# Vision transformer tower: the stacked keys in two tiles of four key chunks each

## The chip, the cores and the metric

The kernel runs on one core of a Trainium2 chip, as a single program. The metric is the device time of one execution in microseconds (us), lower is better. The core has five engines that run side by side, each with its own queue of instructions in a fixed order: TensorE (PE in the profile; its weight loads are PEld), VectorE (DVE), ScalarE (ACT), GpSimd (POOL) and SyncE (SP). SP only issues DMA transfers here, and an instruction that waits on SP holds back all transfers behind it. Instructions wait for each other through semaphores.

## The reference, cut to what matters

Sixteen images of 3 x 512 x 512 are cut into 1024 patches each, and every patch is projected to 256 channels. Then comes one transformer layer with a norm ahead of each part: attention with 8 heads of 32 channels, and a feed-forward part (a shared network, and the two best of four experts). In the attention the keys pass elementwise through a Fourier series of 256 frequencies before they meet the queries:

```python
def _L0_attn_ref(x, w_qkv, w_out, b_out, kan_a, kan_b):
    ...
    q, k, v = (to_heads(q), to_heads(k), to_heads(v))
    k = kan_transform(k, kan_a, kan_b)      # sum_f a_f*sin(f*x) + b_f*cos(f*x), f = 1..256
    scale = HEAD_DIM ** (-0.5)
    dots = jnp.einsum('bhqd,bhkd->bhqk', q, k) * scale
    attn = jax.nn.softmax(dots, axis=-1)
    out = jnp.einsum('bhqk,bhkd->bhqd', attn, v)
    out = out.transpose(0, 2, 1, 3).reshape(b, n, d)
    return out @ w_out + b_out
...
h = _L0_tok_ref(x, L0_tok_W, L0_tok_b)
h = h + _L0_attn_ref(_layernorm(h, axis=-1), ...)
h = h + _L0_ffn_ref(_layernorm(h, axis=-1), ...)
```

All is float32.

## The kernel before, in words

The heads are worked on in pairs: 4 pairs an image, 64 pairs in all, numbered `p` from 0 to 63. The kernel is one long stream without loops on the chip, in which three kinds of work overlap: the Fourier series of the keys of later pairs, the attention of the present pair, and the projections, norms and networks of the images around it.

**The keys.** The angles of an image's keys are written to DRAM (`keys`, tile `ud`) and read back, repeated over partitions, as wave tiles `w` (`load_waves`, two tiles for each of the 32 groups of an image, two transfers of 256 KB for each tile). GpSimd multiplies them by their frequency (`turn_waves`, L1006), ScalarE takes the sine (`sine`, L1016), TensorE mixes them with the coefficients (`mix`, tile `kan`, L1036), VectorE multiplies by the fast waves (`times_fast`, L1050), and TensorE adds up (`add_up`, tile `red`, L1069). After the last sum of a pair, `finish_keys` splits the keys on VectorE into a high and a low part (L615, L616) and stores both to a DRAM tile `kd` with two transfers (L1088).

**The stacked keys.** `stack_keys` (L1098) reads `kd` back into the SBUF tile `k4` of 128 partitions: partitions 0 to 63 hold the high and the low parts of the 32 channels, partitions 64 to 127 the same again, so that one matmul against the stacked queries `q4` (L1115, `stack_queries`, four transfers) forms all products of the parts. In the free dimension `k4` has four rows of 512 columns: two for each head, and of these one for the key chunks 0 to 3 and one for 4 to 7, a chunk being 128 keys. Two transfers of 512 KB fill it, one for each copy. There is one `k4`; it is written again for the next pair once the last score of the present pair has read it.

**The attention.** A pair has two rounds, one for each half of its 1024 queries (`att`, 128 rounds). In a round, for each of eight key chunks `kc`: `score` (L1134) makes two matmuls of 128 keys by 512 queries into a PSUM tile of two banks (`sT`, from the pool `big`, of which there are two, shared with `kan`); `exponential` (L1149) takes the exponential on ScalarE (`es`, five of them); `weigh` (L1167) multiplies with the values and with ones (`av`). After the last chunk VectorE takes the reciprocal and divides (`normalize`, L1191 and L1196). ScalarE changes its table between sine and exponential in each round (L1284 loads the one for the exponential).

**What sets the order.** The order on TensorE is written out in a string, `ORDER`: M is `mix`, R `add_up`, S `score`, W `weigh`, and digits take the next step of one of four chains of the remaining work. The order on the other engines comes from a planner that runs at build time: each step is put in a queue with a cost in us and the steps that it depends on (`put`), and at each point the step that could begin first, by those costs, is laid next (`others`, `heads`). The costs and the `done` times only decide the order of instructions; the waits on the chip come from the tiles that an instruction reads and writes. For `stack_keys` the planner's dependencies are the keys in `kd` and the last score of the pair before; `score` depends on the stacked keys and the queries of its round; `finish_keys` of pair `p` on the stacking of pair `p - 2`, which has read the same one of the two `kd` tiles. Further, a transfer issued on SP waits until the one eight issues before it has landed, because its semaphore is used again.

Of the kernel before, what the change touches and what calls it, by code (L numbers as in the profile page):

```python
# [11 lines left out]
FP = mybir.dt.float32  # L12
# [6 lines left out]
P = 128  # L19
# [4 lines left out]
NT = N // P  # L24
# [17 lines left out]
FPR = mybir.dt.float32r  # L42
# [9 lines left out]
PE, ACT, DVE, POOL, SP = "pe", "act", "dve", "pool", "sp"  # L52
# [38 lines left out]
def plain_path(ctx: ExitStack, tc: tile.TileContext, a: dict, out: bass.AP, verdict: bass.AP):  # L91
# [9 lines left out]
    nc = tc.nc  # L101
# [4 lines left out]
    def pool(name, bufs, space=None):  # L106
        kw = {} if space is None else {"space": space}
        return ctx.enter_context(tc.tile_pool(name=name, bufs=bufs, **kw))

    const = pool("const", 1)  # L110
# [21 lines left out]
    def load(shape, src, name):  # L132
        t = const.tile(shape, FP, tag=name, name=name)
        nc.scalar.dma_start(out=t, in_=src)
        return t
# [33 lines left out]
    half = load([NW5, 2], a["half"], "half")  # L169
    for i in range(4):  # L170
        nc.scalar.dma_start(out=biases[ds((NE + 1) * i, NE), 0, :], in_=a["eb3"])
        nc.scalar.dma_start(
            out=biases[ds((NE + 1) * i + NE, 1), 0, :], in_=a["sb3"].unsqueeze(0)
# [58 lines left out]
    nc.gpsimd.memset(ones32, 1.0)  # L232


    k4 = const.tile([P, 4, 520], FPR, tag="k4", name="k4")
    aT = const.tile([P, 2, N], FP, tag="aT", name="aT")
    hnT = const.tile([P, 2, N], FP, tag="hnT", name="hnT")
    hT_ = const.tile([P, 2, 512], FP, tag="hT", name="hT")
# [13 lines left out]
    done = {}  # L252
# [8 lines left out]
    def put(engine, queue, cost, deps, key, action):  # L261

        queues[engine].setdefault(queue, []).append((cost, deps, key, action))
# [48 lines left out]
    def transfer(took, issue=0.0, ready=0.0):  # L312

        clock[SP] = max(clock[SP], ready) + issue
        now["dma"] = max(now["dma"], clock[SP]) + took
        return now["dma"] + LANDS
# [292 lines left out]
    def split(src, name):  # L609

        hi, lo = (
            rup.tile([P, 512], FPR, tag=tag, name=name + half)
            for tag, half in (("r", "hi"), ("u", "lo"))
        )
        nc.vector.tensor_copy(hi, src)  # L615
        nc.vector.tensor_sub(lo, src, hi.bitcast(FP))  # L616
        return hi.bitcast(FP), lo.bitcast(FP)
# [340 lines left out]
    def load_source(p):  # L958


        def part(j, blk):
            def action():
                if j == blk == 0:
                    sources[p] = srcp.tile([P, 2, 512], INT, tag="src", name="src")
                ud = images[p // NPAIR]["ud"]
                rows = ud[ts(p % NPAIR, 64), :, 0, :].rearrange(
                    "(g j r e) f n -> j r g e f n", j=2, r=2, e=2
                )
                for r in range(2):
                    nc.sync.dma_start(  # L970
                        out=sources[p][ds(64 * j + 32 * blk, 32), r, :],
                        in_=rows[j, r, :, :, :, ts(blk, 512)],
                    )
                landed = transfer(0.4)
                if j == blk == 1:
                    done["source", p] = clock[SP]
                    done["angles", p] = landed

            return action

        deps = rows_of(8 * p) + [("spread", 8 * p - 1) if p > 0 else ("load", 0, 1)]
        for j in range(2):
            for blk in range(2):
                put(SP, "source", 1.4, deps, ("part", p, j, blk), part(j, blk))
# [39 lines left out]
    red = {}  # L1024
# [29 lines left out]
    rows_of_pair = {}  # L1054
# [27 lines left out]
    def finish_keys(p):  # L1082


        def action():
            kd = rows_of_pair["k", p] = kdp.tile([2, P, 512], FP, tag="kd", name="kd")
            for i, x in enumerate(split(rows_of_pair.pop(p), "k")):
                nc.sync.dma_start(out=kd[i], in_=x)  # L1088
            done["kd", p] = transfer(1.4, 1.1, done["keys", p])

        deps = [("red", 4 * p + 3)] + ([("k4", p - 2)] if p > 1 else [])
        put(DVE, "keys", 1.41, deps, ("keys", p), action)

    def stack_keys(p):
        def action():
            src = rows_of_pair.pop(("k", p)).rearrange("i (d q) n -> (i d) q n", q=4)
            for j in range(2):
                nc.sync.dma_start(out=k4.bitcast(FP)[ts(j, 64), :, 0:512], in_=src)  # L1098
            done["stacked", p] = transfer(3.8)

        deps = [("kd", p)] + ([("score", 2 * p - 1, NT - 1)] if p > 0 else [])
        put(SP, "keys", 1.1, deps, ("k4", p), action)

    bands_of_queries = {}

# [23 lines left out]
    def score(att, kc):  # L1129
        def action():  # L1130
            q4 = bands_of_queries[att]
            ps = scores[kc] = big.tile([P, 1024], FP, tag="big", name="sT")
            for s in range(2):
                nc.tensor.matmul(  # L1134
                    out=ps[:, ts(s, 512)],
                    lhsT=k4[:, 2 * s + kc // 4, ts(kc % 4, P)],
                    rhs=q4[:, s, :],
                    start=True,
                    stop=True,
                )  # L1140

        deps = [("stacked", att // 2), ("q4", att)]
        put(PE, "S", 0.47, deps, ("score", att, kc), action)

    def exponential(att, kc):
# [117 lines left out]
    for p in range(total // 8):  # L1263
        load_source(p)
        finish_keys(p)
        stack_keys(p)
    for att in range(ATT):
        stack_queries(att)
        normalize(att)
    for rd in range(B * RI + 2):  # L1270
        groups = range(GS * rd, min(GS * rd + GS, total))
        att = rd - 2
        attends = 0 <= att < ATT
        for g in groups[::2]:
            first = g == groups[0]
            for i, j in ((0, 0), (0, 1), (1, 0), (1, 1), (0, 2), (1, 2)):
                sine(g + i, j, TABLE if first and i == j == 0 else 0.0)
            mix(g)
            mix(g + 1)
            add_up(g // 2)  # L1280

        def table():
            now["table"] = AF.Exp
            nc.scalar.activation(spare[:, 1:2], spare[:, 0:1], AF.Exp)  # L1284

        put(ACT, "fixed", TABLE + 0.2, [], ("table", rd), table)
        for kc in range(NT) if attends else ():
            score(att, kc)
            exponential(att, kc)
            weigh(att, kc)  # L1290
# [590 lines left out]
def vit_layer(tc: tile.TileContext, a: dict, out: bass.AP):  # L1881
    with tc.tile_pool(name="verdict", bufs=1) as vp:
        verdict = vp.tile([1, 1], mybir.dt.int32, tag="verdict", name="verdict")
        plain_path(tc, a, out, verdict)
        bad = tc.nc.values_load(verdict[0:1, 0:1], min_val=0, max_val=1)
        with tc.If(bad > 0):
            general_path(
                tc, *(ap for name, ap in a.items() if name not in PLAIN_ONLY), out
            )
# [149 lines left out]
```

## Time and profile before

| | |
|---|---|
| Time, median of 3 runs | 3939.81 us (3923.31, 3939.81, 3940.42) |
| The profiled execution's own time | 3924.07 us |
| Its span | 3922.5 us, 102737 instructions |
| Granted TensorE clock | 0.994 |
| ScalarE, exponentials L1149 | 1024 of 1022 ns, 1014.3 us |
| TensorE, scores L1134 | 2048 matmuls, 707.6 us |
| GpSimd, waves L1006 (w) | 1024 of 1895 ns, 1923.6 us |
| SP, stacking L1098 | 128 issues of 512 KB, median 592 ns |
| SP, waves L951 | 2048 issues of 256 KB, median 544 ns |
| DMA, mean over the span | 234 GB/s, 80.6% of the engines on SP's queue |

The span is what the profile covers; the time of that execution is 1.6 us more. In a line of the waits, the engine, its line and the tile that it writes come first, then what it waited for, then the total in us, how many times, and the longest. An engine name with a q (SPq) is its sequencer. In the timeline a line has its start, its length, the engine, the line, the operation with its tiles, and in square brackets the idle time of that engine before it and what ended it. The chain that ended last is followed back from the end of the program through whatever released each step.

### The profile page before, as it was taken

How to read it: one execution, taken by the hardware profiler on the slowest of the kernel's cores; microseconds unless marked ns; L12 is line 12 of the kernel's file. 1: busy time of each engine (PE TensorE's matmuls, PEld its weight loads, DVE VectorE, ACT ScalarE, POOL GpSimd, SP SyncE). 2: the span in 40 equal slices, each digit the busy share in tenths (PEclk: the TensorE clock that was granted, in tenths of full speed). 3: DMA queues.
4: the chain of work that ended last, by engine and by line, in shares of the span. 5: the costliest groups of instructions: out<-in, count | busy, mean ns of one | idle time of the engine just before them, and what ended most of it. 6: DMA issues, size and time to landing. Idle time of an engine off the chain costs nothing.

```text
span 3922.5 us, 102737 instructions
## 1 busy us (share of the span) xinstructions
PE 3810.0 (97%) x40337; PEld 1948.9 (50%) x40337; DVE 2531.7 (65%) x4075; ACT 3263.0 (83%) x3939; POOL 3193.6 (81%) x2328
## 2 busy tenths in 40 slices
PE   7899999999999999999999999999999999999998
PEld 4334454554545555455454545545455454544444
DVE  4656757667675766757667675776767767576652
ACT  2788888888888888888888888888888888888983
POOL 3998878788788878879788788878879888888860
PEclk9999999999999999999999999999999999999999
DMA  7987968888787888979889788798878889788860
GB/s 228 281 261 217 278 192 245 259 226 258 220 257 225 237 264 224 259 216 256 235 233 265 212 257 247 224 265 224 262 218 255 247 229 265 216 245 235 221 170 18
DMA packets 587615, 916.51 MB, mean 234 GB/s; under 512 B 58828, under 2 KB 177524, under 8 KB 587124
## 3 DMA queue, kind: packets, MB, share of 16 engines
q1 hardware_dynamic: 580880, 906.98, 80.6%
q8 instruction: 321, 5.26, 0.6%
q10 hardware_dynamic: 6244, 2.88, 0.3%
q14 instruction: 170, 1.39, 0.1%
HBM read 758.64 MB, written 150.99 MB: 232 GB/s over the span
## 4 chain that ended last, share of the span: by engine, by line
PE 66%; DMA 13%; ACT 8%; POOL 5%; DVE 4%; issue 3%; SPq 2%; ACTq 0%; POOLq 0%; DVEq 0%
PE av L1167 17%; PE sT L1134 10%; PE kan L1036 8%; DMA w<-ud 7%; PE red L1069 4%; PE e1p L301 3%; PE tok L301 3%; ACT w L1016 3%; POOL w L1006 3%; PE e3p L301 2%; PE tok L304 2%; DMA k<-kd 2%; PE s1p L301 2%; PE e1p L304 2%; ACT f L1016 2%
## 5 line engine op out<-in xcount | busy, mean ns | idle before, releaser
L1006 POOL TENSOR_TENSOR w<-w,lane 128x1024 int32<-128x1024 int32 x1024 | 1923.6, 1895 | 406.9 <-DMA w<-ud 275.7
L1149 ACT ACTIVATE es<-sT 128x1024 f32<-128x1024 f32 x1024 | 1014.3, 1022 | 357.3 <-PE sT L1134 312.2
L1016 ACT ACTIVATE w<-w 128x1024 f32<-128x1024 int32 x1024 | 1013.4, 1046 | 67.5 <-POOL w L1006 64.3
L1006 POOL TENSOR_TENSOR f<-f,lane 128x1024 int32<-128x1024 int32 x512 | 970.2, 1895 | 102.0 <-DVE f L991 84.8
L1134 PE MATMUL sT<-q,k 128*128 128x512 f32 x2048 | 707.6, 454 | 42.9 <-DMA k<-kd 13.4
L1050 DVE TENSOR_TENSOR f<-kan,f 128x1024 f32<-128x1024 f32 x512 | 605.2, 1214 | 203.1 <-ACT f L1016 116.3
L991 DVE STREAM_SHUFFLE f<-src 128x1024 int32<-128x1024 int32 x512 | 681.3, 1370 | 0.4
L1167 PE MATMUL av<-es,v 128*32 128x256 f32 x8192 | 638.8, 383 | 3.5 <-DVE rc L1208 2.6
L1167 PE MATMUL av<-es,ones 128*32 128x256 f32 x8192 | 630.9, 379 | 0.0
L1036 PE MATMUL kan<-w,coef 64*32 64x512 f32 x8192 | 540.1, 598 | 18.8 <-ACT w L1016 12.6
L1016 ACT ACTIVATE f<-f 128x1024 f32<-128x1024 int32 x512 | 519.0, 1046 | 4.1 <-POOL f L1006 4.1
L1134 PEld LDWEIGHTS sT<-q,k 128*128 128x128 f32 x2048 | 351.2, 190 | 340.0 <-issue 146.0
L1167 PEld LDWEIGHTS av<-es,v 128*32 128x32 f32 x8192 | 235.5, 109 | 343.2 <-issue 236.9
L1167 PEld LDWEIGHTS av<-es,ones 128*32 128x32 f32 x8192 | 267.2, 110 | 176.4 <-issue 1.4
L1191 DVE RECIPROCAL rc<-av 128x256 f32<-128x256 f32 x128 | 224.8, 1756 | 169.5 <-PE av L1167 169.5
L1036 PEld LDWEIGHTS kan<-w,coef 64*32 64x32 f32 x8192 | 129.1, 105 | 313.9 <-issue 133.4
L1069 PE MATMUL red<-f,pack 128*32 128x512 f32 x2048 | 271.0, 602 | 0.0
L301 PE MATMUL tok<-wt,x 128*128 128x256 f32 x768 | 182.1, 389 | 22.1 <-DMA w1s<-in_sW 12.5
L1016 ACT ACT_TABLE_LOAD x128 | 164.2, 1283 | 17.7 <-DMA w<-ud 15.5
L304 PE MATMUL tok<-wt,x 128*32 128x256 f32 x3072 | 178.0, 380 | 0.6 <-DVE h L548 0.6
L301 PEld LDWEIGHTS tok<-wt,x 128*128 128x128 f32 x768 | 147.4, 194 | 57.9 <-DMA w1s<-in_sW 12.4
L513 ACT ACTIVATE hn<-h,less,rstd 128x256 f32<-128x256 f32 x256 | 140.7, 591 | 39.8 <-POOL less L505 39.0
(148 smaller groups left out, 4269.5 us busy)
## 6 DMA issues: line engine op xcount, KB each, us to landing
w<-ud SPq DMA_DIRECT2D x2048, 256.0 KB
q<-qd SPq DMA_DIRECT2D x512, 128.0 KB
k<-kd SPq DMA_DIRECT2D x128, 512.0 KB
x<-in_xT SPq DMA_DIRECT2D x128, 384.0 KB
ud<-u SPq DMA_DIRECT2D x64, 512.0 KB
ud<-ui SPq DMA_DIRECT2D x64, 512.0 KB
src<-ud SPq DMA_DIRECT2D x512, 64.0 KB
qd<-qhi SPq DMA_DIRECT2D x64, 256.0 KB
```

Source lines behind the costliest of these rows:

```text
L301: nc.tensor.matmul(out=out, lhsT=lhsT, rhs=rhs, start=start, stop=stop)
L304: nc.tensor.matmul(out=out[ts(i, 32)], lhsT=lhsT[:, ts(i, 32)], rhs=rhs, start=start, stop=stop)
L991: nc.vector.stream_shuffle(w, sources[g // 8].rearrange("p r n -> p (r n)"), [4 * (g % 8) + i // 8 for i in range(32)],)
L1006: nc.gpsimd.tensor_tensor(w, w, f.to_broadcast([P, N]), ALU.mult)
L1016: nc.scalar.activation(x, w, AF.Sin, scale=TURN * 2.0**-32)
L1036: nc.tensor.matmul(out=ps[ds(64 * j + 32 * blk, 32), ts(r, 512)], lhsT=coef[ts(r, 64)].rearrange("p e f j -> p (e f j)"), rhs=w[ts(r, 64), ...
L1050: nc.vector.tensor_mul(w, kan.pop(g), w)
L1069: nc.tensor.matmul(out=rows_of_pair[p][ts(2 * i + r, 32), :], lhsT=pack[:, ds(PACK0 - 16 * (k % 2) - 2 * (k // 2), 32)], rhs=prod[:, ts(r, ...
L1134: nc.tensor.matmul(out=ps[:, ts(s, 512)], lhsT=k4[:, 2 * s + kc // 4, ts(kc % 4, P)], rhs=q4[:, s, :], start=True, stop=True,)
L1149: nc.scalar.activation(es, scores.pop(kc), AF.Exp, scale=SCALE)
L1167: nc.tensor.matmul(out=acc[0][ts(i, HD), ts(half, 256)], lhsT=ones32 if half else v[:, kc, p % NPAIR, ts(i % 2, HD)], rhs=es[:, ds(512 * ( ...
L1191: nc.vector.reciprocal(rc[0], acc[0][:, 256:512])
```

## The change

`k4` becomes two tiles, one for key chunks 0 to 3 and one for 4 to 7, each with two rows of 512 columns (one for each head). `stack_keys` is called twice for a pair, once for each tile; each call has its own pair of transfers, of 256 KB each, that read every second row of `kd`, its own entry for the planner, and its own condition: the tile may be written again once the last score of the pair before that reads *this tile* is done (chunk 3 or chunk 7 of the pair's second round). A score waits for the tile of its chunk alone. The planner's figures for one call are 0.8 us of SP and 1.9 us of transfer instead of 1.1 and 3.8.

```diff
-    k4 = const.tile([P, 4, 520], FPR, tag="k4", name="k4")
+    k4 = [const.tile([P, 2, 520], FPR, tag=f"k4{i}", name=f"k4{i}") for i in range(2)]
...
-        deps = [("red", 4 * p + 3)] + ([("k4", p - 2)] if p > 1 else [])
+        deps = [("red", 4 * p + 3)] + ([("k4", p - 2, 1)] if p > 1 else [])
         put(DVE, "keys", 1.41, deps, ("keys", p), action)
 
-    def stack_keys(p):
+    def stack_keys(p, half):
+
         def action():
-            src = rows_of_pair.pop(("k", p)).rearrange("i (d q) n -> (i d) q n", q=4)
+            src = rows_of_pair["k", p].rearrange("i (d s h) n -> h (i d) s n", s=2, h=2)[half]
             for j in range(2):
-                nc.sync.dma_start(out=k4.bitcast(FP)[ts(j, 64), :, 0:512], in_=src)
-            done["stacked", p] = transfer(3.8)
-
-        deps = [("kd", p)] + ([("score", 2 * p - 1, NT - 1)] if p > 0 else [])
-        put(SP, "keys", 1.1, deps, ("k4", p), action)
+                nc.sync.dma_start(out=k4[half].bitcast(FP)[ts(j, 64), :, 0:512], in_=src)
+            done["stacked", p, half] = transfer(1.9)
+
+        deps = [("kd", p)] + ([("score", 2 * p - 1, 4 * half + 3)] if p > 0 else [])
+        put(SP, "keys", 0.8, deps, ("k4", p, half), action)
...
-                    lhsT=k4[:, 2 * s + kc // 4, ts(kc % 4, P)],
+                    lhsT=k4[kc // 4][:, s, ts(kc % 4, P)],
...
-        deps = [("stacked", att // 2), ("q4", att)]
+        deps = [("stacked", att // 2, kc // 4), ("q4", att)]
         put(PE, "S", 0.47, deps, ("score", att, kc), action)
...
     for p in range(total // 8):
         load_source(p)
         finish_keys(p)
-        stack_keys(p)
+        for half in range(2):
+            stack_keys(p, half)
```

In the built program the order on TensorE is the same. On SP the two pairs of transfers of a key pair mostly stand next to each other where the one pair stood; in pairs 2 and 3 four wave loads stand between them, in pair 56 an output store, and in pair 58 two stores of queries.

## The prediction

> **What bounds the kernel now.** I read the page first (busy shares, chain that ended last), then the waits of the engines and of SP's queue, then everything that touches the stacked keys, and last the timeline around single key pairs.
>
> From the page of the kernel before:
>
> ```profile
> PE 3810.0 (97%) x40337; PEld 1948.9 (50%) x40337; DVE 2531.7 (65%) x4075; ACT 3263.0 (83%) x3939; POOL 3193.6 (81%) x2328
> ...
> PE 66%; DMA 13%; ACT 8%; POOL 5%; DVE 4%; issue 3%; SPq 2%; ACTq 0%; POOLq 0%; DVEq 0%
> ```
>
> TensorE is idle for only 3922.5 - 3810.0 = 112.5 us of the span (and its busy ends are modelled), so no change to a wait of TensorE can take more than that; a third of the chain runs through other engines and transfers. The loads of the keys (k<-kd) are 2.1% of the chain, ten visits of 6 to 9 us, each a whole time from issue to landing, and not the idle time that they cause.
>
> From the answers on waits, the engines' and then the queue of SP's (us in total, times, longest):
>
> ```profile
> POOL w L1006 <- DMA w<-ud: 275.7, 98, 9.8
> ...
> PE sT L1134 <- DMA k<-kd: 13.4, 10, 2.4
> ```
> ```profile
> SPq L951 <- PE kan L1036: 228.3, 114, 8.9
> ...
> SPq L1098 <- DMA kd<-klo: 121.1, 60, 4.7
> ...
> SPq L951 <- DMA k<-kd: 30.5, 32, 2.8
> ...
> SPq L1098 <- PE sT L1134: 6.5, 2, 4.6
> ```
>
> The last view decides most. The stacking loads (L1098) wait 60 times for their own source, the keys just written to kd, and 2 times for the scores that still read the old keys. So releasing half of k4 earlier starts almost nothing earlier: the loads stand behind kd. What the change can shorten is the landing, since the first scores now need half the bytes.
>
> Where that matters is in the timeline. Pair 22, SP's queue, TensorE and ScalarE:
>
> ```profile
> 1412.39 0.33 SPq L1088 DMA_DIRECT2D kd<-klo  x1
> ...
> 1418.56 1.42 SPq L1098 DMA_DIRECT2D k<-kd  x2
> 1423.22 5.78 SPq L951 DMA_DIRECT2D w<-ud  x8
> ```
> ```profile
> 1428.60 0.70 PE L1134 MATMUL sT<-q,k 128*128 128x512 f32 x2 [1.57 <-DMA k<-kd]
> ...
> 1432.30 0.61 PE L1167 MATMUL av<-es,v 128*32 128x256 f32 x8
> ```
> ```profile
> 1429.23 1.28 ACT L1284 ACT_TABLE_LOAD   x1
> 1430.52 0.20 ACT L1284 ACTIVATE few<-few 128x1 f32<-128x1 f32 x1
> 1430.63 1.98 ACT L1149 ACTIVATE es<-sT 128x1024 f32<-128x1024 f32 x2
> ```
>
> The two loads are issued at 1418.56, land 7.0 and 9.9 us later by the trace's semaphore records, and the first score starts 0.14 us after the second. I set this beside each other of the 64 pairs. In 17 the first score starts within 0.14 us of the landing; the idle time of TensorE before these sums to 21.0 us (the ten that the waits view names, 13.4 us, and seven put down to a VectorE event that fell in the same moment). Eleven of the 17 are every fourth pair, 14 to 54: there four query loads and two query stores stand between the keys' store and the stacking. In the other 47 the keys land 0.5 to 9.6 us before they are needed. The fifth key chunk, first to read the second half, comes 4.2 to 11.4 us after the first.
>
> **What the Trainium skill says.** Its page Perfetto Trace Analysis, section DMA Instruction — HWDGE, says that the profiled window of a DMA instruction leaves the data movement out. The trace agrees: 0.59 us per L1098 row, landings from 4.8 us. DMA: Bandwidth & Descriptors, section Rules for kernel authors, says that two transfers to disjoint halves serialize on the same engines. It agrees too: the second load lands 2.4 to 3.0 us after the first, with 512 KB each, so splitting saves no bandwidth but orders the bytes. Perfetto Trace Analysis, Identifying Dependency Chains, says that an instruction waiting on several engines can have event-semaphore instructions put ahead of it; the trace has 1104 on TensorE at 51 ns each.
>
> **The change part by part.** All sums are against the profiled execution, 3924.07 us (span 3922.5); the median shown is 15.7 us above it, and I carry the difference over.
>
> *First half sooner.* Four loads of 256 KB replace two of 512 KB; each still has rows of 2 KB. At the spacing of 2.4 to 3.0 us per 512 KB, the first pair of halves lands where one old load did, 2.4 to 3.0 us sooner, and that covers every one of the 17 idles (longest 2.35). But what follows has another condition. The first weighting (av) needs the first exponential, which in pair 22 starts 0.11 us after ScalarE has reloaded its table and ends 1431.64; av starts at 1432.30. ScalarE was busy with sines until 1429.2, so a score 1.57 us earlier moves av by at most 0.6. I credit each pair with the smaller of its idle and this slack: pairs 14, 34, 42, 54 nothing, 38 0.15, 50 0.25, 18 0.55, 22 and 46 0.6, 26 1.0, 30 2.35: 5.5 us. Of the six others, pair 0 has 1.3, 1 0.1, 4 none, 8 0.3, 59 1.4, and 63, the last, 1.8: 4.9. Sum 10.4 us; bounds 0 (ScalarE or a later wait takes it all) and 21.0 (all of it arrives).
>
> *Second half.* Lands at most about 1 us after the old second load (two more issues ahead of it), needed 4 us or more later: nothing. In pairs 2 and 3 the planner now lays four wave loads between the halves; at the 8.8 us of pair 2 plus 4 x 1.1 us for their 256 KB each it lands at 13.2 us against a need at 13.7: nothing, at worst 1 us each. In pair 56 an output store and in 58 two query stores come between; those pairs had 6.1 and 1.7 us of slack.
>
> *Two more waits on TensorE per pair.* Chunk 4 now waits for two transfers besides ScalarE: 64 x 2 x 51 ns = 6.5 us at most, none if TensorE was to wait for ScalarE there anyway. I take 3.
>
> *SP's queue.* Two more issues per pair. The nearest row of this size is w<-ud (256 KB, 544 ns median) and the present L1098 row has 592 ns; four at 0.54 with gaps take 2.3 us instead of 1.2. Queued behind are mostly the wave loads that POOL waits for (275.7 us in the view above). In 46 pairs the next issue came 2.3 us or more after the first stacking load began, because it waits for a buffer (in pair 22 4.7 us): covered. In the other 18 it came after 1.2 to 2.25, and the delays sum to 11.7 us. Without a view that shows which of these reach the end I take 3; bounds 0 and 11.7. If the cover were gone everywhere it would be 64 x 1.1 = 70 us.
>
> *The window of transfers.* Every issue on SP waits for the transfer eight issues earlier. Four key loads fill four places with half the bytes each; w loads five to eight behind now wait for quarters at about 3.5, 4.8, 6.1 and 7.4 us, instead of the seventh and eighth for 4.8 and 7.3. They are issued 3 us or later as a rule, so nothing; bounds 0 and 2 us.
>
> *Order elsewhere.* TensorE's instructions stand in the same order; POOL and ScalarE have a few neighbours exchanged, VectorE one: nothing.
>
> Sum: -10.4 + 3 + 3 = -4.4 us, or 3919.7 in the profiled execution and 3935.4, rounded 3936, beside the median.
>
> **The rivals.** About what a measurement of this kernel can tell from no change is 0.5%, 20 us here.
>
> (a) All 21.0 us arrive with no cost: the chain does run through ten of these loads. 3918.8, right at the limit of faster. Against: the table reload of ScalarE, which in most of these pairs ends 2 us after the score.
>
> (b) Slower: the queue of SP. Its place is the first wave loads behind the stacking, its price 1.1 us a pair. If POOL feels it in each pair, 64 x 1.1 - 10 = +60 us, 4000. It decides from where about 0.4 us a pair, some 25 us, gets through. For it: POOL's 98 waits for these loads. Against: 46 pairs have the cover just counted.
>
> (c) The change doesn't do what it says: the release is not what the loads wait for (60 against 2), ScalarE covers the sooner landing, and only the 6 us of costs remain: 3946.
>
> **How the numbers follow.** The small net gain 0.70; (a) 0.10; (b) 0.12; (c) 0.08. Faster by over 0.5%: six tenths of (a), 0.06; slower: most of (b), 0.10; within: 0.84. The ends of the terms give -21 to +22 us, 3919 to 3962; dropping the mishaps that must all meet at the upper end and adding the scatter of the runs shown (17 us), I give 3914 to 3956. (b) in full lies outside.
>
> **What would show it.** Right: the idle of the first score before k<-kd nearly gone from TensorE's waits, in pair 22 the score close behind e3p while the exponential hardly moves; L1098 with 256 rows at about 0.54 us, still waiting for kd; POOL's wait for w<-ud within 10 us of 275.7. Wrong: POOL's wait up by 25 us or more (b); rows of L1098 far dearer; a new wait of sT for k<-kd at the fifth chunk.

## The result and the profile after

The median is 3913.5 us over 13 runs (3907.6 to 3917.7). The kernel before, run beside it 13 times, had 3929.2 us (3923.1 to 3940.4). The ratio is 0.9955 with a 95% interval of 0.9944 to 0.9967: faster by 0.45%, which is inside the 0.5% that I had called hard to tell from no change, and half a microsecond below the low end of my range. The profiled execution took 3913.53 us with a span of 3912.0 us, against 3924.07 and 3922.5 before: 10.5 us less. Of these, 6.6 us are idle time of TensorE (105.9 us after, 112.5 before) and 3.9 us are its busy time (3806.1 after, 3810.0 before), though it does the same number of matmuls. What is behind the second part stands under "TensorE's clock" below.

From the page of the kernel after, busy time, chain and the group of the scores (busy us and mean ns, then the idle time of the engine just before these instructions and what ended most of it):

```profile
PE 3806.1 (97%) x40337; PEld 1946.4 (50%) x40337; DVE 2532.9 (65%) x4075; ACT 3263.2 (83%) x3939; POOL 3196.4 (82%) x2328
...
PE 65%; DMA 12%; ACT 11%; POOL 4%; issue 3%; DVE 3%; SPq 2%; ACTq 0%; POOLq 0%; DVEq 0%
...
L1135 PE MATMUL sT<-q,k 128*128 128x512 f32 x2048 | 706.9, 454 | 25.4 <-ACT es L1150 13.4
...
L1168 PE MATMUL av<-es,v 128*32 128x256 f32 x8192 | 638.8, 383 | 13.6 <-ACT es L1150 11.1
```

The same two groups on the page of the kernel before:

```profile
L1134 PE MATMUL sT<-q,k 128*128 128x512 f32 x2048 | 707.6, 454 | 42.9 <-DMA k<-kd 13.4
...
L1167 PE MATMUL av<-es,v 128*32 128x256 f32 x8192 | 638.8, 383 | 3.5 <-DVE rc L1208 2.6
```

These rows show where the wait went. Ahead of the scores 17.5 us of idle time are gone, and the keys with them. Ahead of the first weighting (av) 10.1 us are new, and what ended most of them is the exponential. Part of the wait has moved one step on, from a transfer to ScalarE; ScalarE's share of the chain went from 8% to 11%.

The engines' waits after (us in total, times, longest) have no row any more in which sT waits for k<-kd (in the second trace of this kernel, taken later, 1.8 us in two waits are left, 0.7 of them at a fifth chunk, in pair 3):

```profile
POOL w L1006 <- DMA w<-ud: 266.7, 92, 9.6
...
PEld av L1168 <- ACT es L1150: 22.5, 15, 1.9
```

The waits of SP's queue:

```profile
SPq L951 <- PE kan L1036: 182.2, 106, 9.1
...
SPq L1099 <- DMA kd<-klo: 114.3, 59, 3.7
...
SPq L951 <- DMA k<-kd: 24.1, 43, 1.2
...
SPq L1099 <- PE sT L1135: 5.2, 2, 3.3
```

The stacking loads still wait for kd, 59 times against 60, and for a score twice. The wave loads (L951) wait for a key load more often than before (43 against 32) but for less time in all (24.1 us against 30.5). The view of the tile k gives the price of one issue (ns, shortest, median and longest):

```profile
L1099 SPq DMA_DIRECT2D k<-kd x256: 512/594/1701, 146.3 to 3807.5; - x128
```

A load of 256 KB costs SP 594 ns, as much as one of 512 KB did (592), not the 544 that I had taken. Pair 22 after, on SP's queue, TensorE and ScalarE:

```profile
1410.63 0.33 SPq L1088 DMA_DIRECT2D kd<-klo  x1
...
1416.74 2.75 SPq L1099 DMA_DIRECT2D k<-kd  x4
1421.63 5.76 SPq L951 DMA_DIRECT2D w<-ud  x8
```
```profile
1424.85 0.59 PE L301 MATMUL e3p<-w3s,s 128*128 128x256 f32 x2
1425.09 0.82 PE L1135 MATMUL sT<-q,k 128*128 128x512 f32 x2
...
1430.10 0.64 PE L1168 MATMUL av<-es,v 128*32 128x256 f32 x8 [1.01 <-ACT es L1150]
```
```profile
1427.64 1.28 ACT L1286 ACT_TABLE_LOAD   x1
1428.93 0.20 ACT L1286 ACTIVATE few<-few 128x1 f32<-128x1 f32 x1
1429.04 1.92 ACT L1150 ACTIVATE es<-sT 128x1024 f32<-128x1024 f32 x2
```

The score now follows e3p with no idle time. ScalarE still ends its sines, reloads its table and begins the exponential at the same place in its own row of work, and av, which before stood behind red without a gap, waits 1.01 us for it. The first score stands 3.51 us earlier in the trace than before (1425.09 against 1428.60) and av 2.20 us (1430.10 against 1432.30). Of this, 1.59 us had been gained in earlier pairs, so this pair adds 0.6 us to av out of its idle time of 1.57.

### The profile page after: what moved, and what is told of

Its sections match the earlier page's. It is cut to its first block, busy times and chain, and to the rows that moved or that the text cites. A ratio compares the mean times of both kernels' runs of the same rounds, so it can differ in the third digit from the quotient of the medians.

```text
span 3912.0 us, 102937 instructions
## 1 busy us (share of the span) xinstructions
PE 3806.1 (97%) x40337; PEld 1946.4 (50%) x40337; DVE 2532.9 (65%) x4075; ACT 3263.2 (83%) x3939; POOL 3196.4 (82%) x2328
## 4 chain that ended last, share of the span: by engine, by line
PE 65%; DMA 12%; ACT 11%; POOL 4%; issue 3%; DVE 3%; SPq 2%; ACTq 0%; POOLq 0%; DVEq 0%
PE av L1168 16%; PE sT L1135 9%; PE kan L1036 9%; DMA w<-ud 6%; ACT w L1016 4%; PE red L1069 4%; PE e1p L301 3%; PE tok L301 3%; PE tok L304 3%; POOL w L1006 2%; ACT f L1016 2%; PE e1p L304 2%; ACT es L1150 2%; PE s1p L301 2%; PE e3p L301 2%
## 5 line engine op out<-in xcount | busy, mean ns | idle before, releaser
L1168 PE MATMUL av<-es,v 128*32 128x256 f32 x8192 | 638.8, 383 | 13.6 <-ACT es L1150 11.1
L301 PE MATMUL tok<-wt,x 128*128 128x256 f32 x768 | 180.8, 387 | 22.0 <-DMA w1s<-in_sW 12.4
L301 PEld LDWEIGHTS tok<-wt,x 128*128 128x128 f32 x768 | 146.4, 193 | 57.3 <-DMA w1s<-in_sW 12.4
```

The source lines that it names most:

```text
L301: nc.tensor.matmul(out=out, lhsT=lhsT, rhs=rhs, start=start, stop=stop)
L1168: nc.tensor.matmul(out=acc[0][ts(i, HD), ts(half, 256)], lhsT=ones32 if half else v[:, kc, p % NPAIR, ts(i % 2, HD)], rhs=es[:, ds(512 * ( ...
```

## The experiments

Three sets were run, each with the kernel before on the same chip: the medians of before are 3924.4 us (50 runs), 3924.4 (57) and 3926.3 (30). The theory is the one of the prediction: what counts is that the bytes of the first four chunks land first; where ScalarE is late, most of it is covered; the release and the costs are worth little. Rivals: it is the earlier start of the loads that pays; it is the smaller transfers, in whatever order; or the two added issues and waits cost something that hides a larger gain.

To see where a kernel gains, I cut each trace at the first scores of pairs 13 and 57 and added up TensorE's idle time before the 64 first scores (us; "split" says whether the keys that count in a stretch come in halves: in the head pairs 0, 1, 4 and 8, in the middle every fourth pair, in the tail pairs 59 and 63). It is referred to below as the table.

| kernel | to pair 13 | 13 to 57 | 57 to end | idle before first scores, by stretch |
|---|---|---|---|---|
| before | 901.6 | 2598.4 | 422.5 | 5.9, 13.6, 3.2 |
| before, second trace | 900.3 | 2603.8 | 421.6 | 5.4, 15.3, 3.9 |
| loads before kd | 903.8 | 2598.3 | 421.5 | 5.9, 14.2, 3.6 |
| last eight pairs | 903.2 | 2599.9 | 416.3 split | 7.4, 12.3, 0.0 |
| other pairs | 903.3 split | 2597.4 | 418.3 | 3.1, 15.1, 2.2 |
| every fourth pair | 903.0 | 2593.5 split | 420.7 | 6.3, 0.0, 3.2 |
| selected pairs | 901.5 split | 2594.4 split | 415.4 split | 2.2, 0.0, 0.0 |
| one tile | 901.6 split | 2594.8 split | 418.2 split | 2.8, 0.0, 0.0 |
| after | 899.7 split | 2594.6 split | 417.7 split | 2.6, 0.0, 0.0 |
| after, second trace | 903.7 split | 2591.6 split | 419.2 split | 3.2, 0.0, 0.0 |
| release held | 898.3 split | 2590.4 split | 417.9 split | 3.5, 0.0, 0.0 |
| halves reversed | 908.2 | 2594.1 | 422.3 | 14.6, 7.5, 5.1 |
| piece first | 899.9 | 2593.7 | 420.4 | 2.5, 0.0, 0.0 |

**Halves reversed.** The change with the second half loaded first. Tiles, sizes and number of transfers are those of the change. Besides the order of the bytes two things change with it: the first transfer now waits for the last score of the pair before, as it did before the change, and what the planner puts between the two halves now delays the half that is needed first.

```diff
-        deps = [("red", 4 * p + 3)] + ([("k4", p - 2, 1)] if p > 1 else [])
+        deps = [("red", 4 * p + 3)] + ([("k4", p - 2, 0)] if p > 1 else [])
...
-        for half in range(2):
+        for half in (1, 0):
             stack_keys(p, half)
```

> Second half of the keys (chunks 4 to 7) is loaded first and the first half after it; tiles, sizes, number of transfers and number of waits are those of the change. Landing theory (the gain is that the first score waits for half the bytes, and the four issues and the added waits cost nothing): the first score again waits for all four transfers, so the gain is gone, 3929 +- 3 us, and the wait of sT for k<-kd is back at about 13 us or more. Cost theory of the prediction (two more issues and two more waits cost 6 us): 3935. If smaller transfers or another order on the queue were the gain, it stays: 3914.

Measured: 3927.4 us (14 runs), ratio 1.0007 (0.9996 to 1.0019). The gain is gone from the total. TensorE's waits have the row again:

```profile
PE sT L1135 <- DMA k<-kd: 25.3, 14, 5.0
```

But it is not gone everywhere. In the table the middle stretch is as short as in the change, and the head and the tail are long. The reason in the head is pair 2, where the planner puts four wave loads between the halves, and what comes after them is now the half that is needed first:

```profile
245.99 1.19 SPq L1099 DMA_DIRECT2D k<-kd  x2
247.28 2.90 SPq L951 DMA_DIRECT2D w<-ud  x4
250.24 1.57 SPq L1099 DMA_DIRECT2D k<-kd  x2
```
```profile
258.61 2.04 PE L1135 MATMUL sT<-q,k 128*128 128x512 f32 x4 [4.98 <-DMA k<-kd]
```

Pair 3 idles 4.68 us and pair 58, with two query stores in the same place, 2.84. In the middle, where the four loads stand together, the idle time before the first scores is 7.5 us over 44 pairs instead of 13.6, on average 0.7 us in each of the eleven pairs that counted (0 to 1.8), and it costs nothing that can be seen. In these eleven pairs the last of the four transfers lands 8.47 us after the first issue, against 9.14 for the last of two before. So the loss stands in the head and the tail, where the order decides, but together with the transfers that came between the halves. In the middle, four smaller transfers did as well in either order, as far as one trace can show it; the rival of the smaller transfers is not excluded there.

**Loads before kd.** The kernel before, but the stacking reads the keys of the pair before, which are long in kd. This kernel leaves out the keys of its own pair from the attention; the same bytes move.

```diff
-            src = rows_of_pair.pop(("k", p)).rearrange("i (d q) n -> (i d) q n", q=4)
+            src = rows_of_pair["k", max(p - 1, 0)].rearrange("i (d q) n -> (i d) q n", q=4)
```

> The kernel before, with its two transfers of 512 KB, but the stacking reads the keys of the pair before (left out: the keys of its own pair in the scores), so it doesn't wait for kd to land; every order is that of the kernel before. Landing theory: the loads begin 2 to 6 us sooner, the first score hardly waits for them any more, and the gain of the change appears without any split: 3913 +- 4 us. If the gain came from the own release or from smaller transfers, nothing changes: 3929.

Measured: 3922.7 us (22 runs), ratio 0.9996 (0.9986 to 1.0005), no gain. I had expected one, and the wait of the scores did not even fall:

```profile
PE sT L1134 <- DMA k<-kd: 18.0, 11, 3.4
```

SP's queue in pair 22 of this kernel says why:

```profile
1415.47 0.33 SPq L1088 DMA_DIRECT2D kd<-klo  x1
1416.37 0.32 SPq L640 DMA_DIRECT2D qd<-qhi  x1
1417.27 0.32 SPq L640 DMA_DIRECT2D qd<-qlo  x1
1418.17 2.65 SPq L1115 DMA_DIRECT2D q<-qd  x4
1421.12 1.76 SPq L1098 DMA_DIRECT2D k<-kd  x2
```

The loads stand behind two query stores and four query loads all the same. Over the eleven pairs they begin 5.47 us after the store of kd instead of 6.07, and the last byte lands later after the issue (9.8 us instead of 9.1): 15.3 us after the store, against 15.2 before. In these pairs the wait named in the queue, kd, is thus not what sets the landing. Starting the loads 0.6 us sooner moved nothing; a start several us sooner, as I had expected it, did not come about and so was not tried. The change itself doesn't start sooner in these pairs either: its first load begins 6.33 us after the store of kd, against 6.07 before, and the half that is needed first has landed 12.1 us after the store, against 15.2. The earlier start is thus not what pays there.

**Every fourth pair, last eight, other pairs, selected pairs.** The split in some pairs alone, the others loaded whole. So that both kinds write the same place, `k4` is one tile here, in the layout of the kernel before.

```diff
+    def stack_whole(p):
+        def action():
+            src = rows_of_pair["k", p].rearrange("i (d q) n -> (i d) q n", q=4)
+            for j in range(2):
+                nc.sync.dma_start(out=k4.bitcast(FP)[ts(j, 64), :, 0:512], in_=src)
...
-        for half in range(2):
-            stack_keys(p, half)
+        if CONDITION:
+            for half in range(2):
+                stack_keys(p, half)
+        else:
+            stack_whole(p)
```

CONDITION is `p % 4 == 2 and p < 56` for every fourth pair (14 pairs), `p >= 56` for the last eight, `p % 4 != 2 and p < 56` for the other 42, and `p % 4 == 2 or p >= 56 or p in (0, 1, 4, 8)` for the selected 26, in which every idle of the prediction's list lies.

> The split only in the 14 pairs 2, 6, 10 ... 54; the others have the two large transfers. Landing theory: the profiled executions put 3.8 of their 10.5 us between pairs 13 and 57, and nearly all of it in these pairs; as a share of 15.7 us that is 5 to 6, so 3923 +- 3. If the gain is spread over all transfers: 14/64 of it, 3926. If it is the release: 3929.

> The split only in the last eight pairs, 56 to 63. Landing theory with the release at pair 63: the profiled executions put 4.8 of their 10.5 us here, so 5 to 7 us of the 15.7: 3923 +- 3. If the gain is spread evenly: 8/64 of it, 3927.

> The split in the 42 pairs below 56 that are not every fourth; the others (2, 6 ... 54 and 56 to 63) have the two large transfers. It carries two thirds of the added issues and waits, and of the late first scores only those of pairs 0, 1, 4 and 8. Landing theory with no cost: ratio 0.999 to 1.000, and as wide a scatter as the kernel before. Cost theory of the prediction: 42/64 of 6 us against 1.7 us of gain, 1.0006. If the gain is that of smaller transfers anywhere: 42/64 of it, 0.997.

> The split in the 26 pairs where the first score waited or the run ends: every fourth pair, 56 to 63, and 0, 1, 4, 8; the other 38 keep the two large transfers. Landing theory: the whole gain of the change, ratio 0.9955 +- 0.0015, with the narrow scatter. With a cost of 6 us for all added issues it would be 3.6 us better than the change, 0.9946. If smaller transfers gain anywhere: 26/64 of it, 0.998.

| split in | us (runs) | ratio | interval |
|---|---|---|---|
| every fourth, 14 pairs | 3913.7 (7) | 0.9963 | 0.9949 to 0.9976 |
| last eight | 3922.2 (20) | 0.9985 | 0.9976 to 0.9994 |
| other 42 pairs | 3919.5 (21) | 0.9989 | 0.998 to 0.9998 |
| selected 26 pairs | 3911.4 (12) | 0.9968 | 0.9957 to 0.9979 |

In the table the idle time is gone in the stretches where each has the split, in the head about half of it. Two things follow. The 42 other pairs have two thirds of all added issues and added waits and the least to gain, and they are not slower: of the 6 us of costs that I had put down for all 64 pairs, 4 would fall to them, and at the upper end of the interval they are still 0.8 us faster, where some 1.7 us of gain was credited to them, which leaves room for about 1 us of cost. And 26 pairs give as much as all 64 (0.9968, against 0.9971 for "one tile" in the same set). How much each part gives alone is less certain: the first three gains add up to 0.63%, twice the whole (0.30%), and only the cautious ends of their intervals (0.24, 0.06 and 0.02%) fit into it.

**One tile.** The change's four transfers in their order, but into one tile that is laid out half by half.

```diff
-    k4 = [const.tile([P, 2, 520], FPR, tag=f"k4{i}", name=f"k4{i}") for i in range(2)]
+    k4 = const.tile([P, 2, 2, 520], FPR, tag="k4", name="k4")
...
-                nc.sync.dma_start(out=k4[half].bitcast(FP)[ts(j, 64), :, 0:512], in_=src)
+                nc.sync.dma_start(out=k4.bitcast(FP)[ts(j, 64), half, :, 0:512], in_=src)
...
-                    lhsT=k4[kc // 4][:, s, ts(kc % 4, P)],
+                    lhsT=k4[:, kc // 4, s, ts(kc % 4, P)],
```

> The change's four transfers, but into one tile, laid out half by half. If what counts is that the score waits for its own half, and waits go by the parts of a tile that are written and read: the change's gain, ratio 0.9955 +- 0.0015. If two tiles were needed for it, every score would wait for all four: 1.000 or above.

Measured: 3913.4 us (12 runs), ratio 0.9971 (0.9961 to 0.9981), and the idle times of the change. The two tiles are not what pays; the waits in this kernel go by the part of a tile that is written and read.

**Piece first, and release held.** Before the change, the loads of the last pair waited for the last score of pair 62 and were issued 6.71 us after the store of kd; after, 2.15 us after it. This is one of the two places where the loads waited for a score, so the gain there could be the release's and not the order's. To give the old release back with the order kept, the first transfer in pairs 56 and 63 writes 16 partitions of the second half, so that it must wait for the last scores on that half.

```diff
+            last = p in (56, 63)
+            if last and half == 0:
+                other = rows_of_pair["k", p].rearrange("i (d s h) n -> h (i d) s n", s=2, h=2)[1]
+                nc.sync.dma_start(out=k4[1].bitcast(FP)[0:16, :, 0:512], in_=other[0:16])
             for j in range(2):
-                nc.sync.dma_start(out=k4[half].bitcast(FP)[ts(j, 64), :, 0:512], in_=src)
+                if last and half == 1 and j == 0:
+                    nc.sync.dma_start(out=k4[1].bitcast(FP)[16:64, :, 0:512], in_=src[16:64])
+                else:
+                    nc.sync.dma_start(out=k4[half].bitcast(FP)[ts(j, 64), :, 0:512], in_=src)
```

> The change, but in pairs 56 and 63, the two where the stacking stood behind a score, a piece of the second half (16 partitions) is loaded ahead of the first half, so that SP must wait for the last chunk as in the kernel before; the first half still lands ahead of the rest. Landing theory: at pair 63 the halves begin as late as before, the first lands some 5.5 us later, and TensorE, which could start the score 6.4 us after that beginning, hardly waits: idle before the first score under 0.3 us. If the own release is what helped there, the idle of 1.8 us is back. The whole time is that of the change within 3 us either way.

Measured: 3914.0 us (18 runs), ratio 0.9974 (0.9965 to 0.9984). It did not test what it should. SP's queue and TensorE around the end of pair 62:

```profile
3804.25 0.61 SPq L1101 DMA_DIRECT2D k<-kd  x1
3804.96 1.75 SPq L1106 DMA_DIRECT2D k<-kd  x2
```
```profile
3808.05 1.18 PE L1142 MATMUL sT<-q,k 128*128 128x512 f32 x4 [1.73 <-DMA k<-kd]
```

The planner may lay the first half of pair 63 between the scores of pair 62, and so it laid the piece ahead of pair 62's last two chunks. These then had to wait 1.73 us for the piece (1.09 us in the same way ahead of pair 56), and they read 16 partitions of the next pair's keys, so this kernel changes part of the computation there. The idle time moved to another score and says nothing on the release. The second version also tells the planner to wait:

```diff
-        deps = [("kd", p)] + ([("score", 2 * p - 1, 4 * half + 3)] if p > 0 else [])
+        until = NT - 1 if p in (56, 63) else 4 * half + 3
+        deps = [("kd", p)] + ([("score", 2 * p - 1, until)] if p > 0 else [])
```

> The change, but in pairs 56 and 63 all stacking loads are put after the last score of the pair before, and the first of them writes 16 partitions of the second half, so that the queue has to wait for that score as it did before the change. The halves still land one after the other. Landing theory (ordering of the bytes is enough): the first half lands about 2.5 us before the second, which covers the 1.8 us; no idle before the first score of pair 63, the stretch from pair 57 to the end within 1.5 us of the change's 417.7, total about 3913.5. Release theory (in the last pairs it is the earlier start that pays): the idle before the first score of pair 63 comes back with 1 to 2.4 us, the stretch from pair 57 grows by as much, total about 3915.5.

Measured: 3912.7 us (6 runs), ratio 0.9972 (0.996 to 0.9984). Now the queue is held, and pair 63 looks so:

```profile
3794.96 0.34 SPq L1088 DMA_DIRECT2D kd<-klo  x1
3801.68 0.61 SPq L1101 DMA_DIRECT2D k<-kd  x1
3802.39 1.19 SPq L1106 DMA_DIRECT2D k<-kd  x2
```
```profile
3807.67 0.59 PE L301 MATMUL e3p<-w3s,s 128*128 128x256 f32 x2
3807.91 1.28 PE L1143 MATMUL sT<-q,k 128*128 128x512 f32 x4
```

The first load begins 6.72 us after the store of kd, as before the change, the first half has landed 5.6 us later, and the score follows e3p without idle time. The tail is as short as in the change (417.9 us). So here the order of the bytes is enough without the own release of each half. By the trace of the change the release by itself would probably have been enough too: there all four transfers of pair 63 have landed 9.37 us after the first issue, and the score starts 10.81 us after it. With the release held, the score starts 6.24 us after the first load.

**The change and the kernel before once more.** The two kernels unchanged, on one chip and with a second trace of each.

> The change itself once more, on the chip of the other experiments. Theory (the change is worth what the two profiled executions show, some 10.5 us of 3924): about 3913.5, ratio 0.9973, within the interval of the same four transfers into one tile (0.9961 to 0.9981). Rival (it is worth the 15.7 us of the first comparison, ratio 0.9955): about 3907 to 3909. In the trace: idle before the first scores under 3 us in all, the stretch from pair 13 to 57 at 2594 to 2595 us.

> The kernel before once more, profiled on this chip, for the scatter of the stretches between two traces of one kernel. If the stretch from pair 13 to 57 is a property of the kernel it is 2598.4 within 0.7 us, and the idle before the first scores 13 to 15 us in it; total about 3924.4, ratio 1.000 within 0.001. If the stretches scatter by 4 us from trace to trace, the gains that were read from them by part mean nothing.

Measured: the change 3913.9 us (7 runs), ratio 0.9970 (0.9959 to 0.9980); before 3927.0 us (22 runs), ratio 0.9996 (0.9988 to 1.0004). In the second trace of before:

```profile
POOL w L1006 <- DMA w<-ud: 279.7, 95, 9.5
...
PE sT L1134 <- DMA k<-kd: 14.5, 9, 3.7
```

The waits repeat, but the middle stretch does not: 2603.8 us against 2598.4, beyond what I had allowed. So no gain by part may be read from one pair of traces. Over all traces of the table it can: the middle has a mean of 2599.6 us in the five kernels with whole keys there (2597.4 to 2603.8) and 2593.2 in the six with split keys (2590.4 to 2594.8), 6.3 less and with no overlap. The tail has 420.9 (five) and 417.4 (six), 3.5 less, where the two groups overlap (418.3 to 422.5, and 415.4 to 419.2). The head has 902.4 (five) and 901.4 (six), 1.0 less within a scatter of 5. The sum is 10.8 us. (The two last rows of the table are left out of these means; in the middle both lie with the split kernels.)

**TensorE's clock.** The traces also hold the clock that TensorE was granted. In the view of the kernel before by windows (start and end, length, TensorE's busy time and matmuls, granted clock, and two columns on the DMA engines that don't matter here) pair 30, whose first score starts at 1902.88 after 2.35 us of idle time, looks so:

```profile
1899.60:1903.00 3.40, 1.05 (x6) 1.00 1.06 229
1903.10:1906.40 3.30, 3.30 (x7) 0.50 1.08 276
1906.50:1909.90 3.40, 3.40 (x30) 1.00 1.08 346
```

Between pairs 13 and 57 the five traces with whole keys have six such stretches of 3.4 us at half the clock, one each and two in the second trace of before. Each begins within 0.6 us of a first score that had waited 1.9 to 2.6 us for its keys. The eight traces with split keys there, halves reversed and piece first among them, have none, and no first score there waited more than 1.83 us. Not every long wait has one: in "other pairs" pair 34 waited 2.16 us at full clock. That the waits bring the half clock about was not tried by itself. A stretch of 3.4 us at half the clock costs at most 1.7 us, so six of them in five traces come to some 2 us a trace, by my estimate. TensorE's busy time in the middle is 2574.9 us on average in the five and 2572.0 in the six. So 2.9 of the 6.3 us are busy time and 3.5 idle time; in the tail it is 1.3 and 2.2, in the head 0.3 and 0.7: together 4.5 and 6.4.

The clock differs from run to run, too, and a higher clock by chance would be a rival to the change. The runs are against it. At a mean clock of 0.995 the median of before is 3923.0 us (51 runs of the three sets), and that of the kernels split where it counts (the change twice, one tile, release held, selected pairs) is 3914.1 (24); at 0.994 it is 3927.5 (63) and 3915.3 (7).

## Why the prediction was wrong

**The gain came out in the sum, in part by luck.** I had credited each pair with the smaller of its idle time and the slack of av: 5.5 us in every fourth pair, 1.7 in the head, 3.2 in the tail, 10.4 in all. The traces show 6.3, 1.0 and 3.5, together 10.8; the two profiled executions differ by 10.5; and four kernels with the split where it counts (the change again, one tile, release held, selected pairs) have ratios of 0.9968 to 0.9972, 11 to 12.6 us. But all that I credited was idle time, and of that only 6.4 us are gone. The other 4.5 us are a shorter busy time of TensorE, for which the prediction has no term: it said that no change to a wait can take more than TensorE's idle time, and left out the granted clock, which fell to half around six of the long waits. The two misses nearly cancel. The rival by which all 21.0 us arrive fits neither the traces nor these four kernels: that idle time did go (from 22.7 us in the table to 2.6), but the time fell by little more than half of it, and the row of av shows where a good part waits now. The interval of the first comparison alone (13 to 22 us) would allow it.

**The mechanism was right in the main.** The loads still wait for kd, the release starts almost nothing earlier, the exponential in pair 22 stays put, and TensorE's wait for the keys is gone but for 1.8 us in one trace. POOL's wait for wave loads is 9 us below its old value in the first trace and 34 below it in the second. What pays is that the keys of the first score land sooner, as every fourth, last eight and selected pairs show: the idle time goes where the keys are split, and the middle and the tail get shorter with it. Release held shows that the order of the bytes is enough in the tail, and one tile that no second tile is needed. In the middle the order and the smaller size of the transfers are not told apart. Two readings were not exact. The loads don't stand behind kd alone: in the busy pairs the stores and loads ahead of them held them nearly as long. And the second load lands 2.2 to 4.3 us after the first over the 64 pairs, not 2.4 to 3.0.

**The step "Two more waits on TensorE per pair" failed.** It took 3 us. The trace after has 65 more event-semaphores on TensorE (1169 against 1104), the kind of instruction that the Trainium skill's page Perfetto Trace Analysis, section Identifying Dependency Chains, describes; the median of one is 51 ns in both traces. But the fifth chunk's first score starts on average 266 ns after the instruction ahead of it, against 270 before. They cost nothing that shows; the term of 3 us was too large by all of it.

**The step "SP's queue" failed.** It took 3 us within bounds of 0 to 11.7. The issues were even dearer than I had put them: those of the stacking take 156.9 us of SP in all, against 76.4 before. But POOL's wait for wave loads did not rise, in any kernel with split keys (212.8 to 274.9 us against 275.7 and 279.7), and the 42 other pairs are not slower. No cost above the lower bound can be seen. With it the rival of a slower queue fell too, and the gain itself speaks against the rival by which only the costs remain.

**The step that carried the sum over to the median failed most.** I had added 15.7 us, the distance between the profiled execution and the median of three runs. That median was high by chance: the kernel before has 3929.2 us with 13 runs beside the change, and 3924.4, 3924.4 and 3926.3 us in the three sets, where its profiled execution (3924.07) is an ordinary run. The miss of 22.5 us (3936 against 3913.5) adds up from this step with 10.6 us (3939.8 to 3929.2), the two costs with 6, rounding with 0.6, and a difference of 5.3 between the 10.4 us credited and the 15.7 of the first comparison. Without the distance and the two costs the sum would have been 3913.7, which is so near to the measured time only because the misses inside the 10.4 us cancel.

**What stays open.** The first comparison has 15.7 us (13 to 22 by its interval), the second 12.4 (7.9 to 16.1), the traces 10.8. The change's median is the same in both comparisons (3913.5, 3913.9); it is the one of before that differs, and the runs don't tell why. How much of the middle's gain needs the order, and how much of the shorter busy time is owed to the clock alone, would need more traces.

## What to carry to other kernels

When a transfer is waited for by work that needs only part of it at first, order its bytes by first use: here it paid without a second tile and without an earlier start, and only up to the next wait, so credit each place with the smaller of its idle time and the slack of the engine that comes next. Look at the granted clock around the longest waits as well: here six of them came with 3.4 us at half the clock, which no sum of idle times holds. Put extra issues at their lower bound when the queue's next issue is already waiting for something else. Forecast the difference against the profiled execution, and add to it no distance to a median of three runs that scatter by more than the change is worth.

## What was not expected of the hardware

Between pairs 13 and 57, TensorE's clock fell to half for 3.4 us around six waits of 1.9 to 2.6 us, and nowhere else. An issue of the stacking has the same price for half the bytes, 594 ns against 592. In the eleven busy pairs the last of four small loads lands sooner after the first issue than the second of two large ones (8.39 us against 9.14, and 8.39 again in the second trace of the change), though the same bytes move; in the 47 pairs that don't wait for their keys it is the reverse (8.21 against 7.73; without the four pairs in which other transfers stand between the halves 7.95 against 7.71). Why was not tried.
